# Cross-attention block on one core: the order of the work on the way into the steady loop

## The chip, the cores and the metric

The kernel runs on one core of a Trainium2 chip. The core has five engines, each with its own in-order instruction stream: TensorE (PE in the profile, matrix products, with its weight loads as PEld), VectorE (DVE), ScalarE (ACT), GpSimd (POOL) and SyncE (SP), which here only issues DMA transfers. GpSimd issues some transfers too. Engines wait for one another through semaphores. The metric is the device time of one execution in microseconds; lower is better.

## The reference

For 16 batches of 1024 rows with 512 features, the reference normalises rows, scales and shifts them by a conditioning vector, and does cross attention with 16 heads of 32 features against 64 context rows of the same batch, then projects and adds the input:

```python
xq = _ada_ln(x_q, t_vec, Wss_q, bss_q)
xkv = _ada_ln(x_kv, t_vec, Wss_kv, bss_kv)
q = (xq @ Wq + bq).reshape(B, Lq, nh, dh)
kv = (xkv @ Wkv + bkv).reshape(B, Lkv, 2, nh, dh)
scores = jnp.einsum('bqhd,bkhd->bhqk', q, k) / jnp.sqrt(jnp.float32(dh))
attn = jax.nn.softmax(scores, axis=-1)
out = jnp.einsum('bhqk,bkhd->bqhd', attn, v).reshape(B, Lq, H)
return x_q + (out @ Wp + bp)
```

`_ada_ln` is a layer norm followed by `(1 + scale) * h + bias`, where scale and bias come from `silu(c) @ W_ss + b_ss`. All is float32.

## The kernel before, in words

The 16 x 1024 rows are cut into 32 blocks of 512 rows, two per batch; a block is called by its number, counted from 0. Each block goes through these steps, each a small Python function that emits the instructions of several engines:

- `load_x(i)` (L140) fetches the rows; `q_stats` (L299) has VectorE take mean and variance; `q_scale` (L308) makes the reciprocal roots. For blocks above 2 (L281 to L288) this is five small ScalarE steps and four small GpSimd steps, "the roots". `hidden` (L328) normalises on ScalarE.
- `turn` (L497) transposes in 32 x 32 tiles on VectorE, and `move` (L510) finishes the transposition with 16 transfers, all on SP's queue or half on GpSimd's.
- Blocks 0 to 3 multiply by a query weight with the batch's scale folded in: `queries(i, o)` (L541), four steps of four matmuls, one PSUM bank each, with a bias add on ScalarE (`queried`, L557; `later=True` leaves that add to a later line). From block 4 on the features are scaled instead (`scale_features`), sums are formed on GpSimd (`feature_sums`), and seven half-size products replace eight (`query_product`, L615; Strassen's scheme). `query_seed` (L642) copies the first product from one bank to another on ScalarE, and product 2 adds onto it.
- `scores(i, z)` (L674) multiplies queries with half of the keys (z = 0 or 1), into two PSUM tiles of two banks each. Each tile is read twice: VectorE takes maxima (L698) and ScalarE copies it to a buffer (L707). The two readings of one tile exclude each other. With `crossed=True` ScalarE starts with the second tile while VectorE starts with the first. There are only two such tiles (`ps_s`), and `mix` and some key and value steps use them also, so the next step that needs one waits until both readings are done.
- `maxima` (L734) spreads the maxima over a full tile `mb` (tag "spread", one buffer), `subtract` (L740) takes them off both halves on GpSimd, `weights` (L746) is the exponential on ScalarE.
- The sums of exponentials: either `total` (L778) adds both halves on GpSimd and `row_total` (L789) sums that on VectorE, or (block 1) `sums` on each half and `halves_total`. `inverse_rows` (L803) takes the reciprocal and sends it to DRAM and back with five transfers on SP; `spread_rows` (L814) spreads what came back.
- `mix` (L839) multiplies with the values, `divided` (L822) divides on VectorE, `row_sums` (L940) forms Strassen's sums on GpSimd. Then follow seven `product` steps (L952) with the output weight into two banks, `added` (L979) after each on VectorE into the residual tile, and `biased` (L927) on ScalarE, which puts a bias into a bank before the products of that bank add to it. Products 1, 6, 5, 3 share one bank and 2, 7, 4 the other.

The schedule is manual: the order of the calls in the body is the order of instructions on every engine. A prologue, then an explicit list of calls for blocks 0 to 3 (L1000 to L1221, "the way in"), then a loop over blocks 4 to 29, then a list for the end. In the way in, the steps of up to five blocks are interleaved. `ring` says which PSUM banks of the four single ones the next steps take in turn; from L1070 on it holds only banks 0 and 1.

A tile with a tag and one buffer is shared in time: the next tile of that tag is written only after the readers of the one before it are through. `s_i_z`, the scores buffers, have the tags big0 to big3: block 3's first half has big2, and so has the sum of block 2's halves, made by `total(2)` with the line

```python
pool, tag = (xpool, "x") if i == NB - 2 else (big, f"big{(i + 1) % 2 * 2}")
```

The query tiles of blocks 2 and 3 share one buffer (tag "qt"), so the bias adds of block 3 can write it only when scores(2,1) has read block 2's.

Of the kernel before, what the change touches and what calls it, by code (L numbers as in the profile page):

```python
# [9 lines left out]
F32 = mybir.dt.float32  # L10
# [5 lines left out]
P = 128  # L16
# [4 lines left out]
def cross_attention_block(  # L21
# [58 lines left out]
    HPC = P // DH  # L80
    TB = 512
    NT = TB // P
# [12 lines left out]
    rpool = ctx.enter_context(tc.tile_pool(name="rpool", bufs=1))  # L95
    opool = ctx.enter_context(tc.tile_pool(name="opool", bufs=1))
# [12 lines left out]
    ring = [0, 1, 2, 3]  # L109
# [189 lines left out]
    def q_stats(i, ts=range(NT), kvb=None):  # L299

        if ts[0] == 0:
            q_mv[i] = small.tile([P, NT + 1, 2], F32, tag="mvq", name=f"mvq_{i}")
        for t in ts:
            row_stats(q_mv[i][:, t, :], x_tiles[i][:, t, :])
        if kvb is not None:
            row_stats(q_mv[i][:, NT, :], ctx_tiles[kvb])

    def q_scale(i, kvb=None):  # L308
        n = NT if kvb is None else NT + 1
        q_rstd[i] = rstd_of(q_mv.pop(i)[:, :n, :], n, "q", i > 2)  # L310
        if kvb is not None:
            kv_rstd[kvb] = (q_rstd[i], NT)
# [228 lines left out]
    def queries(i, o, later=False):  # L541
        xt, b = xt_tiles[i], i // BPB
        w = wq_tiles.get(b, w_q_sb)
        pq = bank(f"pq_{i}_{o}")
        for c in range(NC):
            nc.tensor.matmul(  # L546
                pq.rearrange("p (g n) -> p g n", g=4),
                lhsT=w[:, c, o * P : (o + 1) * P],
                rhs=xt[:, :, c, :],
                start=(c == 0),  # L550
                stop=(c == NC - 1),
            )
        pq_tiles[i, o] = pq
        if not later:
            queried(i, o)
# [115 lines left out]

    s_tiles, m_tiles = {}, {}

    def scores(i, z, crossed=False):  # L674

        kt, qt = k_tiles[i // BPB], qt_tiles[i]
        pss = [ps_s.tile([P, 2, TB], F32, tag="s", name=f"ps_{i}_{z}_{e}") for e in range(2)]
        for r in range(HPC):
            rows = slice(32 * r, 32 * r + 32)
            for c in range(NC):  # L680
                nc.tensor.matmul(  # L681
                    pss[r // 2][32 * c : 32 * c + 32, r % 2, :],
                    lhsT=kt[rows, c, z * HK : (z + 1) * HK],
                    rhs=qt[rows, c, :],
                    start=True,
                    stop=True,
                )
        if z == 0:
            m_tiles[i] = small.tile([P, 2, HPC, NJ], F32, tag="m2", name=f"m2_{i}")
        if i < NB - 1:  # L690
            pool, tag = big, f"big{i % 2 * 2 + z}"
        else:

            pool, tag = ((hpool, "ht"), (qpool, "xt"))[z]
        s_sb = pool.tile([P, HPC, TB], F32, tag=tag, name=f"s_{i}_{z}")

        def maximum(e):
            nc.vector.tensor_reduce(  # L698
                m_tiles[i][:, z, 2 * e : 2 * e + 2, :],
                pss[e].rearrange("p r (j a) -> p r j a", a=32),  # L700
                AX.X,
                ALU.max,
                apply_transpose=True,
            )

        def copied(e):
            nc.scalar.copy(s_sb[:, 2 * e : 2 * e + 2, :], pss[e])  # L707


        for step in (  # L710
            ((maximum, 0), (copied, 1), (maximum, 1), (copied, 0))
            if crossed
            else ((maximum, 0), (copied, 0), (maximum, 1), (copied, 1))
        ):
            step[0](step[1])
        s_tiles[i, z] = s_sb
# [33 lines left out]
    def sums(i, z):  # L750
        if z == 0:
            l_tiles[i] = small.tile([P, 2, HPC, NJ], F32, tag="l2", name=f"l2_{i}")
        nc.vector.tensor_reduce(  # L753
            l_tiles[i][:, z],
            s_tiles[i, z].rearrange("p r (j a) -> p r j a", a=32),
            AX.X,
            ALU.add,
            apply_transpose=True,
        )
# [17 lines left out]

    def total(i):  # L778

        if i == 0:  # L780

            t = opool.tile([P, HPC, TB], F32, tag="ot", name="sum_0")
        else:
            pool, tag = (xpool, "x") if i == NB - 2 else (big, f"big{(i + 1) % 2 * 2}")
            t = pool.tile([P, HPC, TB], F32, tag=tag, name=f"sum_{i}")
        nc.gpsimd.tensor_tensor(t, s_tiles[i, 0], s_tiles[i, 1], ALU.add)  # L786
        sum_tiles[i] = t
# [139 lines left out]
    def biased(i, k):  # L927

        b = b_first if k == 2 else b_diff
        k = acc_bank(i, 1 if k == 2 else 7)  # L930
        acc[k] = bank(f"pp_{i}_{k}", k)
        b = b.unsqueeze(1).to_broadcast([P, 2, HO])
        nc.scalar.copy(acc[k].rearrange("p (t h) -> p t h", t=2), b)
# [6 lines left out]
    def row_sums(i, n):  # L940

        tt = nc.gpsimd.tensor_tensor
        if n == 0:
            s1_tiles[i] = opool.tile([P, HC, HT], F32, tag="s1", name=f"s1_{i}")
            tt(s1_tiles[i], half_rows(i, 1, 0), half_rows(i, 0, 0), ALU.subtract)
            tt(half_rows(i, 1, 0), half_rows(i, 1, 1), half_rows(i, 1, 0), ALU.subtract)  # L946
        else:
            s2_tiles[i] = opool.tile([P, HC, HT], F32, tag="s2", name=f"s2_{i}")
            tt(s2_tiles[i], half_rows(i, 1, 1), s1_tiles[i], ALU.subtract)  # L949
            tt(half_rows(i, 0, 1), half_rows(i, 0, 1), s2_tiles[i], ALU.subtract)  # L950

    def product(i, n):  # L952

        rows, cols = {
            1: (lambda: half_rows(i, 0, 0), half_weights(0, 0)),
            2: (lambda: half_rows(i, 0, 1), half_weights(1, 0)),
            3: (lambda: half_rows(i, 1, 1), WT[:, 3]),
            4: (lambda: half_rows(i, 0, 1), half_weights(1, 1)),
            5: (lambda: s1_tiles.pop(i), WT[:, 0]),
            6: (lambda: s2_tiles.pop(i), WT[:, 1]),  # L960
            7: (lambda: half_rows(i, 1, 0), WT[:, 2]),
        }[n]
        rows = rows()
        k = acc_bank(i, n)
        if n == 2:
            acc[k] = bank(f"pp_{i}_{n}", k)
        for t in range(2):
            for c in range(HC):

                nc.tensor.matmul(  # L970
                    acc[k][:, t * HO : (t + 1) * HO],
                    lhsT=rows[:, c, t * P : (t + 1) * P],
                    rhs=cols[:, c, :],
                    start=n == 2 and t == 0 and c == 0,
                    stop=c == HC - 1,
                    skip_group_check=True,
                )

    def added(i, n):  # L979

        m, o = {1: (0, 0), 2: (0, 0), 6: (0, 1), 7: (1, 1), 5: (1, 1), 4: (0, 1), 3: (1, 0)}[n]
        r = r_tiles[i][:, 2 * m : 2 * m + 2, o * HO : (o + 1) * HO]
        k = acc_bank(i, n)
        a = acc[k].rearrange("p (t h) -> p t h", t=2)
        if i == NB - 1:

            for ts in ((0,), (1,)) if n == 3 else ((0, 1),):
                ts = slice(ts[0], ts[-1] + 1)
                nc.vector.tensor_add(r[:, ts, :], a[:, ts, :], r[:, ts, :])
                if n in (2, 3, 4, 5):  # L990
                    dst = rows_of(out, i)[:, 2 * m : 2 * m + 2, o * HO : (o + 1) * HO]
                    nc.sync.dma_start(dst[:, ts, :], r[:, ts, :])
            return
        nc.vector.tensor_add(r, a, r)  # L994
        if n in (3, 4):
            nc.sync.dma_start(
                rows_of(out, i)[:, 2 * m : 2 * m + 2, :], r_tiles[i][:, 2 * m : 2 * m + 2, :]
            )
# [68 lines left out]
    weights(0, 1)  # L1067
    total(0)
    move(3)
    ring[:] = [0, 1]  # L1070
    scores(1, 0, crossed=True)
    queries(2, 0)
    row_total(0)
    inverse_rows(0)
    load_x(5)
# [1 line left out]
    scores(1, 1)  # L1077
    maxima(1)
    subtract(1)
    queries(2, 1)  # L1080
    queries(2, 2)
    biased(0, 2)
    mix(0)
    spread_rows(0)
    divided(0)
    queries(2, 3)
    weights(1, 0)
    queries(3, 0, later=True)
    row_sums(0, 0)
    q_stats(4, (0, 1))  # L1090
    sums(1, 0)
    q_stats(4, (2, 3), kvb=2)
    weights(1, 1)
    product(0, 1)
    added(0, 1)
    product(0, 2)
    row_sums(0, 1)
    q_scale(4, kvb=2)
    query_weight_sums()


    scores(2, 0, crossed=True)
    added(0, 2)
    biased(0, 3)
    queries(3, 1, later=True)
    scores(2, 1)
    queried(3, 0)
    queried(3, 1)
    hidden(4, range(NT))
    maxima(2)  # L1110
    subtract(2)
# [34 lines left out]
    row_sums(1, 1)  # L1146
    q_stats(5, (3,))
    q_scale(5)
    row_total(2)
    inverse_rows(2)  # L1150
    load_residual(2)


    scores(3, 0, crossed=True)
    scale_features(4)
    feature_sums(4)
    product(1, 7)
# [161 lines left out]
    y, z = NB - 2, NB - 1  # L1319
# [134 lines left out]
```

## Time and profile before

| what | value |
|---|---|
| runs | 1042.91, 1044.82, 1045.44 us; median 1044.82 us |
| the profiled execution | 1045.25 us, of which the profiled span is 1043.3 us |
| TensorE busy | 1021.9 us, 98% of the span |
| VectorE, GpSimd, ScalarE busy | 854.4, 781.5, 610.9 us |
| mean granted TensorE clock | 0.998 |
| DMA | 147.63 MB moved, 142 GB/s |

A line of TensorE's waits reads: what waited (engine, tile, line), what it waited for (engine, tile, line), total us, number of times, the longest. A line of the timeline reads: start in us from the span's start, duration in us, engine, line, operation, output and inputs, shape, count; in brackets the idle time of the engine before it and what ended it. Rows of one kind that follow each other are merged into one. The line of the stretches gives the stretch, its sum, TensorE's busy time and count, the granted clock as a share of full speed, the share of DMA time and GB/s.

The page calls a busy TensorE busy even where its matmuls wait inside a merged row, so a row that takes longer than another of the same kind has to be looked at.

### The profile page before, as it was taken

Reading aid. Unit: us, or ns where it says so; the run is one execution under the profiler, and the core shown is the slowest. Engines: PE = TensorE matmul, PEld = TensorE weight load, DVE = VectorE, ACT = ScalarE, POOL = GpSimd, SP = SyncE. Lnnn points to the kernel's source line nnn. Section 1 sums busy time; section 2 is a strip of 40 time slices with the busy share of each in tenths; the row PEclk is TensorE's granted clock in tenths of the full one; section 3 lists DMA queues with packets and bytes.
Section 4 is the critical chain, followed back from the end, with each engine's and each line's share of the span. In section 5 each row is a group of like instructions: output and inputs, shape, how many; then the busy total and the mean of one; then the engine's idle time right before and its main releaser. Section 6 shows DMA issues by size and latency. Waiting matters only on the chain.

```text
span 1043.3 us, 22968 instructions
## 1 busy us (share of the span) xinstructions
PE 1021.9 (98%) x9058; PEld 760.0 (73%) x9058; DVE 854.4 (82%) x1159; ACT 610.9 (59%) x945; POOL 781.5 (75%) x502
## 2 busy tenths in 40 slices
PE   5999999999999999999999999999999999999998
PEld 3635686778777777777777787778787778777746
DVE  5798977987788977987878878898778997776795
ACT  3666755665567655766556666567557665565530
POOL 0479795887868868888668986688876886977861
PEclk9999999999999999999999999999999999999999
DMA  9851555444454434554335454344354444335122
GB/s 341 250 162 54 150 180 154 128 136 139 154 156 143 125 117 140 166 164 132 117 112 161 154 159 133 110 139 155 137 163 118 141 141 131 102 123 161 45 87 84
DMA packets 103499, 147.63 MB, mean 142 GB/s; under 512 B 33464, under 2 KB 34640, under 8 KB 103392
## 3 DMA queue, kind: packets, MB, share of 16 engines
q1 hardware_dynamic: 102368, 144.08, 43.5%
q0 software_dynamic: 1024, 2.10, 0.9%
q8 instruction: 71, 1.16, 0.5%
q14 instruction: 36, 0.29, 0.1%
HBM read 79.02 MB, written 34.60 MB: 109 GB/s over the span
## 4 chain that ended last, share of the span: by engine, by line
PE 91%; DVE 5%; DMA 1%; ACT 1%; POOL 1%; issue 1%; SPq 0%; DVEq 0%; ACTq 0%; POOLq 0%
PE pp L970 35%; PE pq L633 33%; PE po L855 6%; PE ps L681 6%; PE pq L546 4%; PE pv L434 3%; PE pk L398 3%; DVE m L698 1%; DMA x<-in_x_dram 1%; DVE bs L263 1%; DVE ht L503 0%; POOL s L742 0%; DVE lt L791 0%; ACT s L748 0%; DVE l L753 0%
## 5 line engine op out<-in xcount | busy, mean ns | idle before, releaser
L742 POOL TENSOR_TENSOR s<-s,mb 128x2048 f32<-128x2048 f32 x62 | 281.3, 4564 | 171.3 <-DVE mb L729 167.2
L707 ACT COPY s<-ps 128x1024 f32<-128x1024 f32 x128 | 129.4, 1012 | 112.7 <-DVE m L698 69.5
L698 DVE TRANSPOSE_TENSOR_REDUCE m<-ps 128x32 f32<-128x1024 f32 x128 | 150.8, 1215 | 31.1 <-PE ps L681 29.5
L970 PE MATMUL pp<-w_p_sb,ot 128*128 128x256 f32 x744 | 171.0, 379 | 0.9 <-DVE ot L835 0.5
L994 DVE TENSOR_TENSOR r<-pp,r 128x512 f32<-128x512 f32 x210 | 136.3, 670 | 32.1 <-PE pp L970 25.0
L663 ACT ACTIVATE qt<-pq,bias_t 128x256 f32<-128x256 f32 x224 | 92.6, 464 | 116.0 <-PE pq L633 113.3
L970 PEld LDWEIGHTS pp<-w_p_sb,ot 128*128 128x128 f32 x744 | 141.0, 190 | 21.8 <-issue 1.7
L748 ACT ACTIVATE s<-s 128x2048 f32<-128x2048 f32 x64 | 122.3, 1911 | 41.8 <-POOL s L742 40.0
L786 POOL TENSOR_TENSOR sum<-s,s 128x2048 f32<-128x2048 f32 x30 | 136.2, 4541 | 5.5 <-ACT s L748 5.5
L970 PEld LDWEIGHTS pp<-WT,s 128*128 128x128 f32 x496 | 90.6, 191 | 57.0 <-issue 35.2
L970 PE MATMUL pp<-WT,s 128*128 128x256 f32 x496 | 124.2, 394 | 0.2 <-POOL s L949 0.2
L970 PE MATMUL pp<-WT,ot 128*128 128x256 f32 x496 | 117.6, 380 | 1.0 <-POOL ot L946 0.6
L633 PE MATMUL pq<-xt_sums,wq_sums 128*128 128x256 f32 x448 | 108.5, 385 | 0.0
L633 PEld LDWEIGHTS pq<-xt_sums,wq_sums 128*128 128x128 f32 x448 | 82.9, 190 | 32.8 <-issue 21.8
L633 PE MATMUL pq<-xt,wq_sums 128*128 128x256 f32 x448 | 106.6, 381 | 0.0
L633 PE MATMUL pq<-xt,w_q_sb 128*128 128x256 f32 x448 | 106.0, 379 | 0.3 <-ACT pq L645 0.3
L970 PEld LDWEIGHTS pp<-WT,ot 128*128 128x128 f32 x496 | 93.9, 190 | 16.6 <-POOL ot L946 2.3
L324 ACT ACTIVATE x<-x,rstdq 128x512 f32<-128x512 f32 x128 | 96.6, 807 | 1.9 <-DVE rstdq L294 1.9
L670 DVE TENSOR_TENSOR qt<-pq,qt 128x256 f32<-128x256 f32 x112 | 42.0, 417 | 66.5 <-PE pq L633 66.1
L633 PEld LDWEIGHTS pq<-xt,w_q_sb 128*128 128x128 f32 x448 | 85.0, 190 | 13.1 <-ACT xt L573 0.8
L263 DVE BATCH_NORM_STATS2 bs<-x 128x6 f32<-128x512 f32 x128 | 86.9, 679 | 7.3 <-DMA x<-in_x_dram 7.3
L633 PEld LDWEIGHTS pq<-xt,wq_sums 128*128 128x128 f32 x448 | 83.5, 190 | 11.9 <-issue 1.4
(128 smaller groups left out, 1583.4 us busy)
## 6 DMA issues: line engine op xcount, KB each, us to landing
x<-in_x_dram SPq DMA_DIRECT2D x32, 1024.0 KB, 5.9
r<-in_x_dram SPq DMA_DIRECT2D x32, 1024.0 KB, 5.5
out_dram<-r SPq DMA_DIRECT2D x60, 512.0 KB, 3.7
xt<-ht SPq DMA_DIRECT2D x464, 64.0 KB, 2.0
wss_q<-in_L_xcond_Wss_q_dram SPq DMA_DIRECT2D x2, 1024.0 KB, 9.1
ctx<-in_ctx_dram SPq DMA_DIRECT2D x8, 256.0 KB, 3.1
wss_kv<-in_L_xcond_Wss_kv_dram SPq DMA_DIRECT2D x2, 1024.0 KB
w_kv_sb<-in_L_xcond_Wkv_dram SPq DMA_DIRECT2D x1, 2048.0 KB
```

The costliest lines, as they stand in the source:

```text
L263: nc.vector.bn_stats(bs, r)
L324: nc.scalar.activation(dst, src, AF.Identity, bias=rstd[:, 1, j : j + 1], scale=rstd[:, 0, j : j + 1])
L633: nc.tensor.matmul(qa[k][:, m * HT : (m + 1) * HT].rearrange("p (g n) -> p g n", g=2), lhsT=a[:, c, m * P : (m + 1) * P], rhs=x[:, :, c, : ...
L663: nc.scalar.activation(dst, src, AF.Identity, bias=bq_t[:, o : o + 1])
L681: nc.tensor.matmul(pss[r // 2][32 * c : 32 * c + 32, r % 2, :], lhsT=kt[rows, c, z * HK : (z + 1) * HK], rhs=qt[rows, c, :], start=True, s ...
L698: nc.vector.tensor_reduce(m_tiles[i][:, z, 2 * e : 2 * e + 2, :], pss[e].rearrange("p r (j a) -> p r j a", a=32), AX.X, ALU.max, apply_tra ...
L707: nc.scalar.copy(s_sb[:, 2 * e : 2 * e + 2, :], pss[e])
L742: eng.tensor_tensor(s_tiles[i, z], s_tiles[i, z], mb_tiles[i], ALU.subtract)
L748: nc.scalar.activation(p, p, AF.Exp, scale=SCALE)
L786: nc.gpsimd.tensor_tensor(t, s_tiles[i, 0], s_tiles[i, 1], ALU.add)
L970: nc.tensor.matmul(acc[k][:, t * HO : (t + 1) * HO], lhsT=rows[:, c, t * P : (t + 1) * P], rhs=cols[:, c, :], start=n == 2 and t == 0 and ...
L994: nc.vector.tensor_add(r, a, r)
```

## The change

Nothing that is computed changes. All edits lie in the way in, between about 59 and 160 us of the span:

1. `queries(2, 0)` is called ahead of `scores(1, 0)`, and so still takes a bank of the ring of four; the ring is then set to `[1, 0]`. The other three query steps of block 2 follow one call earlier each, the last of them ahead of `mix(0)`.
2. `sums(1, 0)`, one VectorE step, comes behind the maxima of `scores(2, 0)`, and the statistics of block 4 are made in one go.
3. `added(0, 2)` comes ahead of `row_sums(0, 1)` and the maxima of `scores(2, 0)`; the roots of block 4 come behind `query_weight_sums` and behind the copies of `scores(2, 0)` and the bias copy `biased(0, 3)`.
4. The bias adds of block 3's first two query steps come ahead of the copies of `scores(2, 1)`, through the new argument `first`.
5. `total(2)` puts the sum of block 2's halves into the buffer "spread" and not big2.
6. `row_total(2)`, `inverse_rows(2)` and `load_residual(2)` come behind `scores(3, 0)`.

```diff
-    def scores(i, z, crossed=False):
+    def scores(i, z, crossed=False, first=()):
...
+        for step in first:
+            queried(*step)
         if z == 0:
...
     def total(i):
-        if i == 0:
-            t = opool.tile([P, HPC, TB], F32, tag="ot", name="sum_0")
+        if i in (0, 2):
+            pool, tag = (opool, "ot") if i == 0 else (rpool, "spread")
+            t = pool.tile([P, HPC, TB], F32, tag=tag, name=f"sum_{i}")
...
     move(3)
-    ring[:] = [0, 1]
+    queries(2, 0)
+    ring[:] = [1, 0]
     scores(1, 0, crossed=True)
-    queries(2, 0)
+    queries(2, 1)
     row_total(0)
...
     subtract(1)
-    queries(2, 1)
     queries(2, 2)
+    queries(2, 3)
     biased(0, 2)
     mix(0)
     spread_rows(0)
     divided(0)
-    queries(2, 3)
     weights(1, 0)
     queries(3, 0, later=True)
     row_sums(0, 0)
-    q_stats(4, (0, 1))
-    sums(1, 0)
-    q_stats(4, (2, 3), kvb=2)
+    q_stats(4, range(NT), kvb=2)
     weights(1, 1)
     product(0, 1)
     added(0, 1)
     product(0, 2)
+    added(0, 2)
     row_sums(0, 1)
-    q_scale(4, kvb=2)
     query_weight_sums()
     scores(2, 0, crossed=True)
-    added(0, 2)
     biased(0, 3)
+    q_scale(4, kvb=2)
+    sums(1, 0)
     queries(3, 1, later=True)
-    scores(2, 1)
-    queried(3, 0)
-    queried(3, 1)
+    scores(2, 1, first=((3, 0), (3, 1)))
     hidden(4, range(NT))
...
     q_scale(5)
+    scores(3, 0, crossed=True)
     row_total(2)
     inverse_rows(2)
     load_residual(2)
-    scores(3, 0, crossed=True)
     scale_features(4)
```

## The prediction

> **What bounds the kernel now.** I read the page's busy shares first, then TensorE's waits, then the clock by stretches, then the timelines of the stage that the edits touch (59 to 160 us).
>
> ```profile
> span 1043.3 us, 22968 instructions
> ...
> PE 1021.9 (98%) x9058; PEld 760.0 (73%) x9058; DVE 854.4 (82%) x1159; ACT 610.9 (59%) x945; POOL 781.5 (75%) x502
> ```
>
> TensorE is busy 98% of the span, so a change can only win its idle time, 21.4 us, or slow periods of its clock. About 10.5 us of the idle lie before 11.3 us and 2.4 after 175 us. TensorE's waits between 40 and 175 us are what is left for this change:
>
> ```profile
> PE ps L681 <- ACT s L707: 1.9, 2, 1.3
> PE ps L681 <- DVE vt L447: 1.2, 1, 1.2
> PE pq L546 <- ACT qt L568: 0.5, 1, 0.5
> PE pp L970 <- issue: 0.4, 1, 0.4
> PE pq L633 <- ACT pq L645: 0.3, 1, 0.3
> ```
>
> The columns are total us, times, longest. The second wait is also followed by a slow clock (TensorE by stretches: us, busy, clock, DMA share, GB/s):
>
> ```profile
> 158.00:159.00 1.00, 0.00 (x0) 1.00 0.17 17
> ...
> 160.00:161.00 1.00, 1.00 (x10) 0.50 0.85 301
> ...
> 162.00:163.00 1.00, 1.00 (x3) 0.50 1.02 365
> 163.00:164.00 1.00, 1.00 (x6) 0.97 1.11 246
> ```
>
> The granted clock is halved from about 159.6 to 163.0 us: 3.4 us at half speed, 1.7 us of work lost. It is the only such place (the mean clock is 0.998).
>
> The stage where most edits meet, TensorE's timeline, then VectorE's, then ScalarE's:
>
> ```profile
> 115.76 1.14 PE L681 MATMUL ps<-qt,kt 32*32 32x512 f32 x32
> 117.33 1.97 PE L970 MATMUL pp<-WT,ot 128*128 128x256 f32 x8 [0.42 <-issue]
> ...
> 122.37 1.17 PE L681 MATMUL ps<-qt,kt 32*32 32x512 f32 x32 [1.34 <-ACT s L707]
> ...
> 127.53 1.99 PE L633 MATMUL pq<-xt,w_q_sb 128*128 128x256 f32 x8 [0.34 <-ACT pq L645]
> ```
>
> ```profile
> 117.30 2.28 DVE L791 TRANSPOSE_TENSOR_REDUCE lt<-sum 128x64 f32<-128x2048 f32 x1
> 119.61 0.55 DVE L806 RECIPROCAL lt<-lt 128x64 f32<-128x64 f32 x1
> 120.08 2.31 DVE L698 TRANSPOSE_TENSOR_REDUCE m<-ps 128x32 f32<-128x1024 f32 x2
> ```
>
> ```profile
> 125.04 1.95 ACT L707 COPY s<-ps 128x1024 f32<-128x1024 f32 x2
> 126.88 0.59 ACT L645 COPY pq<-pq 128x512 f32<-128x512 f32 x1
> ```
>
> VectorE has no pause from 115.9 to 141.8 us: there it is as full as TensorE.
>
> **Hand-over times**, read from rows. A scores step keeps TensorE 1.07 us; the maxima of its first bank can start 1.19 us after its first matmul (87.19 to 88.38), the copy of its second after 1.35 (43.34 to 44.69). A whole query product takes 3.63, its bias add may start 3.74 after its start (97.15 to 100.89). A half-size product takes 1.73 to 1.83; its addition may start about 1.9 after its start. Maxima 1.2, copy 1.0, spread 2.31 each. Maxima and copy of one bank exclude each other.
>
> **First part, 59.6 to 97 us: queries(2,·) around scores(1,·).** Now scores(1,0) starts at 59.62 and the next step at 61.96: 2.34 us instead of 1.07, because the last bias add of block 1 (60.16, behind an exponential on ScalarE) is late. Then scores(1,1) waits 0.57 for copies. Changed: queries(2,0) covers 59.62 to 63.25 (its features and weights are there by 53); scores(1,0) 63.25; queries(2,1) to 67.95; its copies end at 66.7 and maxima at 66.8, so scores(1,1) goes on. Gain 1.27+0.57 = 1.84. Without that cover the copies (66.7) against 64.3 would cost 2.4. queries(2,2) and (2,3) reach 76.08, mix(0) 78.36, queries(3,0) 81.9, where block 3's features (last issue 71.6, 2.6 to land) are ready. VectorE's division of block 0 starts at 78.39 (mix start + 2.31) instead of 78.26: 0.13, hidden under queries(3,0). Products 1 and 2 run from 81.9 to 85.45, scores(2,0) 85.45, queries(3,1) 86.52 to 90.15, scores(2,1) 90.15.
>
> Order on VectorE: five statistics (0.8 each) to 84.65, added(0,1) and now added(0,2) to 86.2, maxima 86.64 to 89.2 (the second waits for the copy that follows weights(1,1), 87.0 to 88.0), then sums(1,0), now behind them, to 91.5, maxima of scores(2,1) to 93.9, spread to 96.5 (98.2 before). ScalarE: copies to 89.0, b_diff copy 89.6, five roots to 90.9; queried(3,0) and (3,1) have to wait for scores(2,1) to have read the same buffer, 91.5 to 92.75, then the copies to 94.9. So queries(3,2) finds its bank free and starts at 94.8 instead of 97.15: the 0.47 wait goes too, **−2.3** in all. On GpSimd the weight sums now come ahead of the roots' four small steps (1.1): hidden(4) may start at 96.45, not 94.9, and turn(4) needs it only at 101.6, so that costs nothing. subtract(2) starts at 96.6 (98.35 before).
>
> **Second part, 97 to 119 us: sum_2 in the "spread" buffer, row_total(2) behind scores(3,0).** VectorE is 1.65 ahead: sums(1,1) ends at 100.0, the reciprocal at 100.85; its way through DRAM takes 4.66 as now (102.5 to 107.16), to 105.5; division of block 1 at 107.9. TensorE: mix(1) 103.69, queries(3,3) to 109.5, products to 113.4, scores(3,0) 113.45. product(1,7) needs the b_diff copy (114.85) and row_sums on GpSimd (subtract(2) to 105.65, weights(2,1) 107.75, total 112.4, two steps: 115.0), so it starts at 115.2 and scores(3,1) at 118.8. In the old form the copy into big2 waited for row_total(2) to read that buffer (119.66) and scores(3,1) could start only at 122.37. Here the lead is 3.6.
>
> **Third part, where that lead is lost.** row_total(2) and its reciprocal (2.78) have not left VectorE, they stand behind. The first maxima start at 115.0; the second bank's wait for its copy, which is behind five roots on ScalarE (115.2 to 116.35): 117.4 to 118.6, 1.2 idle. Then row_total and reciprocal to 121.35, added(1,7) and (1,6) to 122.6, maxima of scores(3,1) to 125.0, second copy 126.0, seed copy 126.55. Queued behind row_total are thus two additions, four maxima and through them the seed that query_product(4,2) waits for: it starts at 126.6 instead of 127.53, **−0.95**. TensorE has query_product(4,1) from 119.9, waits 1.0 for added(1,6), runs product(1,5), and waits 2.1 for the seed: 3.1 us idle where there were 1.7. The moved inverse_rows also sends five small transfers and the load of r_2 later on SP's queue: first transfer at 121.5 instead of 120.19; it lands behind x_6 (issued 117.0, 5.9 us: 123), the rest by 127.4; spread_rows(2) wants them at 128.2, so 0.8 is to spare. Block 4's move is 16 issues, 106 to 116.7, landed by 118.9, in time for its scaling; r_2 lands by 134, wanted at 139.
>
> **Fourth part, 127 to 160 us.** TensorE has no wait till scores(4,0), VectorE keeps its 0.95: turn(5) ends at 139.45, load_x(7) lands as now 6.0 later, statistics of block 7 at 145.5 to 148.7, one addition to 149.45. row_total(3) had to wait 1.33 for GpSimd; now subtract(3) begins at 127.7 (130.49 before), the sum is ready at about 149.1, and no wait is left. From row_total's start to the last value tile is 7.1 us (151.72 to 158.85): 156.55. The second half of scores(4,0), wanted at 156.3, starts at 156.7 instead of 159.0: **−2.3** (0.95 and two effects of 0.4 to 0.9: the gap shrinks from 1.2 to 0.4).
>
> **The clock.** The gap at 158 is gone, so I take the slow window away: **−1.7**. From 163 us on TensorE sets the pace again and a lead at scores(4,1) is kept: VectorE had 4.4 us idle there. Sum: −2.3−1.7 = −4.0, bounds −1.0 (both clock terms bad) and −5. The profiled execution took 1045.25 us (1.95 around its span), so 1041.25, **1041.3**. Against the runs' median, 1044.82, this is −0.34%; those runs lie between 1042.91 and 1045.44, and the lowest may be one without a slow window.
>
> The rule that speaks against it: this trace halves the clock after a gap of 1.2 us (beside scores, whose matmuls are 32x32), but not after 1.34 at 122.37. [...]
>
> **The rivals.** (a) The new idle time halves the clock: 1042.65, 1041.8 to 1043.8, chance 0.28. For: the row at 160. Against: the larger gap without it at 122. (b) The gain isn't there: the roots ahead of the copy hold VectorE longer than 1.2 us, the seed comes at 127.5 as now and the gap and slow clock at 158 stay: 1045.2, chance 0.12. For: VectorE's full row. Against: it is fed 1.65 to 2.3 earlier. (c) Slower: the small transfers of inverse_rows(2) are caught behind bulk loads, spread_rows(2) blocks VectorE's queue with the division of block 2, turn(5) and load_x(7) behind it. Each us beyond 128.2 counts; with the lead of 4.0 used up and 3.1 more, it decides from about 7 us of lateness: 1048.5, chance 0.14. For: such a transfer took 4.8 us behind a load at 120. Against: 9 us from reciprocal to use now.
>
> **How the numbers follow.** The main case has 0.46, with its own range 1040.2 to 1042.4. A measurement of this kernel tells about 0.3%, 3.1 us: faster is below 1041.7, slower above 1048.0. Faster: 0.40 of the main case and 0.04 of (a): 0.44. Same: 0.06+0.24+0.12 = 0.42. Slower 0.14. The range leaves out (c) and some of each end: 1040.0 to 1045.4.
>
> **What would show it.** Right: queries(3,2) near 94.8; scores(3,1) near 118.8 with no wait for L791's buffer; a wait of about 2 us before query_product(4,2) near 126.6; scores(4,0) without a 1.2 us gap; no halved clock at 160. Wrong if the clock row shows a halved stretch between 124 and 132, if spread_rows(2) waits for its transfer, if row_total(3) still waits for GpSimd, or if TensorE shows new waits after 165 us.

## The result and the profile after

| | before | changed |
|---|---|---|
| median of 13 runs each, us | 1045.17 (1042.88 to 1046.55) | 1040.9 (1039.77 to 1043.3) |
| ratio to before, with 95% interval | | 0.9965 (0.9956 to 0.9975) |
| profiled execution, us | 1045.25, span 1043.3 | 1040.31, span 1038.5 |

The changed kernel is faster by 0.35%. The forecast was 1041.3 us. The executions of the kernel before lie in two groups, about 1043 and 1045.5 us (here 5 and 8 of 13), so a ratio to it depends on how many fall into each; the experiments show that it is the clock of TensorE (a mean of 0.998 and less in the upper group, of 0.999 and more in the lower).

After the change TensorE is busy for 1019.3 of 1038.5 us. Its waits from 40 to 175 us:

```profile
PE pq L633 <- ACT pq L645: 1.8, 1, 1.8
PE pp L976 <- POOL ot L952: 0.6, 1, 0.6
PE pq L633 <- ACT xt L573: 0.3, 1, 0.3
```

All the old waits for a scores tile are gone; what has grown is the wait for the seed copy (L645), 1.8 us instead of 0.3. The first part, TensorE before: the two steps of scores(1,·), of which the first is cut in two by a wait, and queries(3,2):

```profile
59.62 1.05 PE L681 MATMUL ps<-qt,kt 32*32 32x512 f32 x6
60.88 1.13 PE L681 MATMUL ps<-qt,kt 32*32 32x512 f32 x26 [0.21 <-ACT qt L568]
...
66.22 1.18 PE L681 MATMUL ps<-qt,kt 32*32 32x512 f32 x32 [0.57 <-ACT s L707]
...
97.15 3.70 PE L546 MATMUL pq<-xt,wq 128*128 128x512 f32 x8 [0.47 <-ACT qt L568]
```

The same after, without a wait:

```profile
61.78 1.14 PE L684 MATMUL ps<-qt,kt 32*32 32x512 f32 x32
...
66.48 1.14 PE L684 MATMUL ps<-qt,kt 32*32 32x512 f32 x32
...
93.31 3.60 PE L546 MATMUL pq<-xt,wq 128*128 128x512 f32 x8
```

TensorE's timeline in the stage where the edits meet, to be held against the four lines shown of before:

```profile
112.46 1.14 PE L684 MATMUL ps<-qt,kt 32*32 32x512 f32 x32
...
117.86 1.14 PE L684 MATMUL ps<-qt,kt 32*32 32x512 f32 x32
...
121.52 1.99 PE L976 MATMUL pp<-WT,s 128*128 128x256 f32 x8
125.34 1.99 PE L633 MATMUL pq<-xt,w_q_sb 128*128 128x256 f32 x8 [1.83 <-ACT pq L645]
```

VectorE at the same time, and ScalarE's copies and seed:

```profile
114.09 1.22 DVE L703 TRANSPOSE_TENSOR_REDUCE m<-ps 128x32 f32<-128x1024 f32 x1
116.29 1.25 DVE L703 TRANSPOSE_TENSOR_REDUCE m<-ps 128x32 f32<-128x1024 f32 x1 [0.98 <-ACT s L712]
117.47 2.27 DVE L797 TRANSPOSE_TENSOR_REDUCE lt<-sum 128x64 f32<-128x2048 f32 x1
...
120.24 1.22 DVE L1000 TENSOR_TENSOR r<-pp,r 128x512 f32<-128x512 f32 x2
```

```profile
122.65 2.14 ACT L712 COPY s<-ps 128x1024 f32<-128x1024 f32 x2 [1.33 <-DVE m L703]
124.69 0.59 ACT L645 COPY pq<-pq 128x512 f32<-128x512 f32 x1
```

The row sum of block 2 (L797) stands between the two pairs of maxima, and ahead of it VectorE waits 0.98 us for a copy. Both were forecast. At scores(4,0) the gap between the two halves of the step is down from 1.22 us, before:

```profile
156.69 1.09 PE L681 MATMUL ps<-qt,kt 32*32 32x512 f32 x16
159.00 1.42 PE L681 MATMUL ps<-qt,kt 32*32 32x512 f32 x16 [1.22 <-DVE vt L447]
```

to 0.16 after:

```profile
154.51 1.09 PE L684 MATMUL ps<-qt,kt 32*32 32x512 f32 x16
155.75 1.09 PE L684 MATMUL ps<-qt,kt 32*32 32x512 f32 x16 [0.16 <-PE ps L684]
```

The idle time of these rows understates the gap. In a step without a gap the second half starts 0.45 us after the first (e3 below, and every other scores step of the changed kernel); at scores(4,0) it starts 2.31 us after it before and 1.24 in this profile. So the second half is late by 1.9 us before and still by 0.8 after.

The clock stays full both there and beside the wait for the seed (columns as in the prediction):

```profile
124.00:126.00 2.00, 0.66 (x3) 1.00 0.17 16
...
156.00:160.00 4.00, 4.00 (x31) 1.00 0.85 295
```

**A ruler for small differences.** From the first `mix` behind scores(4,1) on, the starts of successive `mix` steps were compared over eight profiles of different kernels: the same 29.2, 29.6, 32.8 and 33.0 us recur, step by step within 0.2 us. What differs from one profile to the next outside the way in is the start (the first scores step began at 42.0 to 43.6 us) and the last stores (from the last mix step to the end 21.4 to 23.4 us over seven of them). So I count from the first matmul of scores(0,0) to the first one of three later steps. This takes the start and the end out, and leaves the way in:

| kernel | to queries(3,2) | to query_product(4,2) | to scores(4,1) | clock halved in the profile | executions with a halved stretch | ratio to before |
|---|---|---|---|---|---|---|
| before | 53.81 | 84.19 | 121.98 | yes, 3.4 us | 23 of 60 | 1 |
| changed | 51.25 | 83.28 | 118.36 | no | 0 of 13 | 0.9965 |
| e5, changed again | 51.25 | 82.69 | 117.31 | no | 0 of 8 | 0.9973 |
| e1, edits 1 to 4 | 51.25 | 81.91 | 118.03 | no | 0 of 8 | 0.9974 |
| e2, edits 5 and 6 | 54.00 | 85.38 | 120.23 | no | 0 of 11 | 0.9990 |
| e9, edit 1 | 52.83 | 83.21 | 120.96 | yes, 3.4 us | 9 of 10 | 0.9996 |
| e10, edits 2 to 4 | 53.20 | 83.48 | 119.61 | no | 9 of 10 | 1.0003 |
| e3, before, gap closed | 53.82 | 84.20 | 118.17 | no | 0 of 9 | 0.9975 |
| e4, changed, roots later | 51.25 | 81.68 | 117.10 | no | 0 of 5 | 0.9965 |
| e8, e4 and values earlier | 51.25 | 81.50 | 115.47 | no | 0 of 5 | 0.9958 |
| e6, gap made longer | 53.84 | 84.22 | 124.49 | yes, 6.8 us | 4 of 4 | 1.0041 |
| e7, seed made later | 51.26 | 84.13 | 120.53 | yes, 3.4 us | 8 of 10 | 0.9991 |

The last column but one is read from the mean granted clock of each execution. In the profile of before the clock is 0.50 from 159.64 to 163.06 us; such a stretch of 3.41 us takes 1.7 of some 1043 us, or 0.0016, off the mean, so 0.998 and less are counted as halved. The clock also falls behind the last matmul of the program: in the profile of the changed kernel that one ends at 1034.81 us, and the clock is 0.95 from 1037.00 to 1038.50. The eight profiles without a halved stretch have a mean of 0.999 or 1.000. The 60 executions of before are those on the three chips of the experiments.

For a halved stretch of 3.41 us I take off 1.7, half of its length: an estimate, which the rows bear out (the second half of scores(4,0) and the product behind it take 1.42 and 3.32 us in before, 1.09 and 2.00 in e1 at full clock, 1.65 less). So before without it is 120.28. The two profiles of the changed kernel are 1.9 and 3.0 us below that. Three profiles of the kernel before agree within 0.04 us (121.95 to 121.99), the two of the changed kernel differ by 1.05.

### The profile page after: what moved, and what is told of

It is laid out like the page before. It is cut to its first block, busy times and chain, and to the rows that moved or that the text cites. A ratio compares the mean times of both kernels' runs of the same rounds, so it can differ in the third digit from the quotient of the medians.

```text
span 1038.5 us, 22968 instructions
## 1 busy us (share of the span) xinstructions
PE 1019.3 (98%) x9058; PEld 759.5 (73%) x9058; DVE 854.9 (82%) x1159; ACT 610.6 (59%) x945; POOL 780.9 (75%) x502
## 3 DMA queue, kind: packets, MB, share of 16 engines
q8 instruction: 72, 1.18, 0.5%
## 4 chain that ended last, share of the span: by engine, by line
PE 84%; DVE 7%; DMA 3%; POOL 3%; ACT 1%; issue 1%; SPq 0%; DVEq 0%; POOLq 0%
PE pp L976 34%; PE pq L633 33%; PE po L861 6%; PE ps L684 6%; PE pv L434 2%; PE pk L398 2%; DMA x<-in_x_dram 2%; DVE m L703 1%; DVE bs L263 1%; DVE l L758 1%; DVE vb L823 1%; DVE lt L797 1%; DMA vr<-ltd 1%; DVE ot L841 1%; DVE r L1000 0%
```

## The experiments

### Which edits carry the gain

**e1_order_only.** The changed kernel with edits 5 and 6 taken back:

```diff
-        if i in (0, 2):
+        if i == 0:
...
-    scores(3, 0, crossed=True)
     row_total(2)
     inverse_rows(2)
     load_residual(2)
+    scores(3, 0, crossed=True)
```

> The changed kernel with its edits 5 and 6 undone: the sum of block 2 is in big2 again, and row_total(2) with its transfers stands ahead of scores(3,0) again. Theory A (the order edits 1 to 4 carry the gain, and VectorE sets the pace between 110 and 126 us, so moving row_total only moves the wait): the copies of scores(3,0) wait for row_total(2) again, scores(3,1) waits about 1.2 us for them, but VectorE loses no time waiting for a copy; from queries(3,2) to query_product(4,2) it takes about 30.9 us (32.0 in the changed kernel, 30.4 in the one before), and the time is 0 to 1 us below the changed kernel's, near 1040. Rival B (the buffer and the later row_total carry a good part): 1042.5 to 1043.5.

Measured: 0.9974 (0.9964 to 0.9983), median 1041.23 us against 1043.81 of before on that chip. TensorE waits at scores(3,1) again, but the seed is there earlier than in the changed kernel (84.19 − 81.91 = 2.3 us won, against 0.9 and 1.5 in its two profiles); from queries(3,2) to query_product(4,2) it takes 30.66 us. TensorE's waits:

```profile
PE ps L684 <- ACT s L712: 1.3, 1, 1.3
PE ps L684 <- DVE vt L447: 1.2, 1, 1.2
...
PE pq L633 <- ACT pq L645: 0.3, 1, 0.3
```

The time is that of the changed kernel, not the 1 us below it which I allowed for: the gap at scores(4,0) is back (1.18 us) and uses the earlier seed up. Edits 1 to 4 alone are worth the whole change, as far as intervals of about 1 us to either side can tell.

**e2_buffer_only.** Edits 5 and 6 alone on the kernel before:

```diff
-        if i == 0:
...
+        if i in (0, 2):
+            pool, tag = (opool, "ot") if i == 0 else (rpool, "spread")
...
+    scores(3, 0, crossed=True)
     row_total(2)
     inverse_rows(2)
     load_residual(2)
...
-    scores(3, 0, crossed=True)
```

> The kernel before with edits 5 and 6 alone: the sum of block 2 in the spread buffer, row_total(2) behind scores(3,0). Theory A: the wait of 1.34 us before scores(3,1) goes, but the seed copy comes 1.3 us later, because row_total now stands between the two pairs of maxima and VectorE also waits for a copy; from queries(3,2) to query_product(4,2) 31.7 us instead of 30.4. The gap at scores(4,0) shrinks since TensorE is late itself, so the time is 1043.5 to 1045.5, by whether the clock is then halved. Rival B: 1042 to 1043, 2 to 3 us faster than before.

Measured: 0.9990 (0.9982 to 0.9999), median 1043.34. The wait before scores(3,1) is gone, and the seed is 1.2 us later (85.38 against 84.19; expected 1.3): the moved row sum only changes what TensorE waits for. TensorE comes later to scores(4,0) and finds no idle time there, and none of 11 executions has a halved stretch, against 8 of 23 of before on that chip. That is the whole of the small rest: the 15 executions of before at full clock have a median of 1043.44, e2 one of 1043.34, and to scores(4,1) the two take the same, 120.23 and 120.28.

**e9_queries_only.** Edit 1 alone on the kernel before:

```diff
-    ring[:] = [0, 1]
+    queries(2, 0)
+    ring[:] = [1, 0]
     scores(1, 0, crossed=True)
-    queries(2, 0)
+    queries(2, 1)
...
-    queries(2, 1)
     queries(2, 2)
+    queries(2, 3)
...
     divided(0)
-    queries(2, 3)
```

> The kernel before with edit 1 alone (queries(2,0) ahead of scores(1,0), the other three one call earlier). From the first matmul of scores(0,0) to that of queries(3,2) it took 53.8 us before and 51.3 in the changed kernel. Theory (the two groups of order edits need each other: TensorE gains 1.8 us at scores(1,0) and scores(1,1), but VectorE's old order takes part of it back at scores(2,0) and scores(2,1)): 52.8 to 53.0 here, and to scores(4,1) 119.3 us, against 120.3 before without the halved clock and 118.0 with all of edits 1 to 4. Rival (edit 1 does it all): 51.5 to 52.0, and 118.3.

Measured: 52.83 us to queries(3,2), 1.0 of the 2.6 that the changed kernel wins there; and 119.26 us to scores(4,1) when the 1.7 of its halved stretch are taken off 120.96. The old order behind TensorE's takes back the rest: scores(2,1) waits 0.88 us for the copies of scores(2,0). They stand behind block 4's roots on ScalarE, which waited 0.75 us for the statistics that VectorE makes behind sums(1,0):

```profile
90.28 1.47 PE L681 MATMUL ps<-qt,kt 32*32 32x512 f32 x32 [0.88 <-ACT s L707]
```

The ratio, 0.9996 (0.9985 to 1.0008), shows no gain, but the clock hides it: 9 of 10 executions are halved, against 8 of 19 of before on that chip. At halved clock the medians are 1043.72 and 1045.48 us.

**e10_rest_only.** Edits 2 to 4 alone: e1 with the four query steps where they were before.

```diff
-    queries(2, 0)
-    ring[:] = [1, 0]
+    ring[:] = [0, 1]
     scores(1, 0, crossed=True)
-    queries(2, 1)
+    queries(2, 0)
...
     subtract(1)
+    queries(2, 1)
     queries(2, 2)
-    queries(2, 3)
...
     divided(0)
+    queries(2, 3)
```

> The kernel before with edits 2 to 4 alone (sums, additions, roots, bias adds ahead of the copies; the queries stay). Theory: only the wait of 0.47 us before queries(3,2) goes, the distance from scores(0,0) to queries(3,2) is 53.2 to 53.4; the spread of block 2's maxima comes as before, since scores(2,1) comes as before, so to scores(4,1) it takes 119.9 to 120.3 us without a halved clock. Rival (edits 2 to 4 do it all): 51.5 to 52.0, and 118.3.

Measured: 53.20 us to queries(3,2), and 119.61 to scores(4,1), a little better than expected; 1.0003 (0.9990 to 1.0016). Here too 9 of 10 executions are halved, though not the profiled one; the nine have a median of 1044.51 against 1045.48 of before at halved clock. The singles win 1.0 and 0.7 us of way in (120.28 − 119.26 and 120.28 − 119.61), both together 2.25 (e1: 120.28 − 118.03), each read from one profile: edit 1 brings scores(2,0) and scores(2,1) earlier on TensorE, and only the new order on VectorE can take them up.

**e4_roots_later.** The changed kernel, and the five roots of block 5 behind the copies of scores(3,0):

```diff
-    q_scale(5)
     scores(3, 0, crossed=True)
+    q_scale(5)
     row_total(2)
```

> The changed kernel with one more move: the roots of block 5 stand behind the copies of scores(3,0) on ScalarE. Theory A: VectorE's wait of 1.0 us for the copy of scores(3,0)'s second tile goes, the seed copy and all of VectorE's work up to load_x(7) come 1.0 us earlier; from queries(3,2) to query_product(4,2) 31.0 us instead of 32.0, the time 1.0 us below the changed kernel's, about 1039.9. Rival (TensorE's 1.8 us wait for the seed is covered later anyhow): the wait shrinks to 0.8 but the time stays at 1040.9.

Measured: the 0.98 us of VectorE are gone (its two maxima are one row again), and the seed comes 1.0 to 1.6 us earlier than in the two profiles of the changed kernel:

```profile
114.95 2.35 DVE L703 TRANSPOSE_TENSOR_REDUCE m<-ps 128x32 f32<-128x1024 f32 x2
117.22 2.27 DVE L797 TRANSPOSE_TENSOR_REDUCE lt<-sum 128x64 f32<-128x2048 f32 x1
```

TensorE's wait for the seed shrinks to 1.16 us, but a gap of 0.50 opens at scores(4,0), whose second half is 1.1 us late (it starts 1.58 after the first), and the ratio, 0.9965 (0.9953 to 0.9977), cannot be told from the changed kernel's. So whether the 1.0 us shows in the time is left open.

### The gap, the seed and the clock

**e3_gap_closed.** The kernel before with one move:

```diff
+    value_products(2, spare("pv_2"))
+    value_tiles(2)
     turn(6, range(NT))
     load_x(8)
-    value_products(2, spare("pv_2"))
-    value_tiles(2)
```

> The kernel before with one move: value_products(2) and value_tiles(2) are called ahead of turn(6), so VectorE frees the second PSUM tile about 2.4 us earlier and scores(4,0) has no gap of 1.2 us. Theory (the gap beside the scores step makes the clock fall): no halved stretch near 160 us in the profile, and the median falls by 1.2 for the gap and up to 1.7 for the clock, to 1042.3 to 1043. Rival (the halved stretch has another cause, and comes by chance): 1.2 us less only, 1044, with halved stretches still there in the longer runs.

Measured: 0.9975 (0.9965 to 0.9985), median 1041.35; scores(4,0) runs without a gap and the clock is full. To query_product(4,2) it is the kernel before (84.20 us), to scores(4,1) it is 2.1 us below it, on top of the halved stretch. That is more than the 1.2 us that were expected for the gap, and the median is below the 1042.3 to 1043 forecast: the second half of the step now starts 0.45 us after the first, not 2.31, so the gap had cost 1.9 and not the 1.2 of its row. At full clock before has 1043.44 on that chip, again 2.1 above. This one move, which the change does not make, is worth about as much as the change.

**e6_gap_at_scores.** The kernel before, with two transposes of block 6 done twice, which makes VectorE 1.2 us later at the value tiles:

```diff
-        for t in ts:
+        for t in [*ts, 2, 3] if i == 6 else ts:
             nc.vector.transpose(
```

> The kernel before with turn(6) transposing its last two tiles twice, 1.2 us more on VectorE ahead of the value tiles: the gap inside scores(4,0) becomes 2.4 us. Theory (idle time beside the scores step lets the clock fall): the clock is halved for 3.4 us right after it, and the time is 1.2 us above the kernel before plus up to 1.7 for the executions of that one that keep their clock, so 1.2 to 2.9. [...]

Measured: slower, 1.0041 (1.0025 to 1.0057), 1048.31 against 1043.42 us. The gap is 2.41 us, and the clock is halved not for 3.4 us but for 6.8, from 159.2 to 166.0 (columns as before):

```profile
156.37 1.09 PE L681 MATMUL ps<-qt,kt 32*32 32x512 f32 x16
159.87 1.96 PE L681 MATMUL ps<-qt,kt 32*32 32x512 f32 x16 [2.41 <-DVE vt L447]
```

```profile
159.00:160.00 1.00, 0.13 (x8) 0.58 0.00 0
160.00:161.00 1.00, 1.00 (x16) 0.50 0.21 55
...
165.00:166.00 1.00, 1.00 (x4) 0.51 0.57 109
```

1.2 us more on VectorE cost 4.9 by the medians, more than the 1.2 to 2.9 expected, since before is mostly at full clock there (11 of 18 executions) and every execution of e6 is halved, three of four at a mean clock of 0.997.

**e7_gap_at_seed.** The changed kernel, the first maxima of scores(3,1) taken twice:

```diff
             step[0](step[1])
+            if (i, z) == (3, 1) and step == (maximum, 0):
+                step[0](step[1])
```

> The changed kernel with the first maxima of scores(3,1) taken twice, 1.2 us more on VectorE ahead of the seed copy: TensorE's wait for the seed grows from 1.8 to 3.0 us, among full-size matmuls. VectorE's chain sets the end of the way in, so the time is about 1.2 us above the changed kernel's. [...]

Measured: 0.9991 (0.9982 to 1.0001), median 1043.08, which is 1.8 above the changed kernel on that chip, where about 1.2 was expected. The clock falls in 8 of 10 executions; these have a median of 1043.29, and the two at full clock took 1042.54 and 1042.58: halving seems to cost less than 1.7 us of the time here, and with two executions that is not settled. With 3.11 us of wait for the seed the clock is halved from 128.2 to 131.6 us:

```profile
127.04 2.69 PE L633 MATMUL pq<-xt,w_q_sb 128*128 128x256 f32 x8 [3.11 <-ACT pq L645]
```

```profile
128.00:129.00 1.00, 1.00 (x4) 0.59 1.05 399
...
130.00:131.00 1.00, 1.00 (x4) 0.50 0.05 18
```

**e11_before_again, e12_before_again.** The kernel before, unaltered, for two more profiles.

> The kernel before, unaltered, for another profile. The executions of it lie in two groups, about 1043 and 1045.5 us. Theory (the gap of 1.2 us at scores(4,0) lets the clock fall only in some executions): either a halved stretch of 3.4 us at about 159 and a time near 1045.5, or full clock and a time near 1043; the gap is there in both. Rival: a halved stretch elsewhere, or none in an execution of 1045.5.

> As e11_before_again: one more sample of the kernel before. The gap at scores(4,0) is 1.2 us; halved clock and about 1045.5 us, or full clock and about 1043 us.

Measured: 1045.54 and 1045.57 us, both with the gap (1.19 and 1.21 us) and a halved clock. In e11 the stretches show it from 159.3 us on, for 3.4 us; in e12 the mean clock is 0.998, and the second half of scores(4,0) and the product behind it take 1.34 and 3.38 us (1.09 and 2.00 in e1). With the first one that is three of three, all in the upper group; no profile caught one of the lower group. But the mean clock of every execution shows that the groups are the clock's: on the three chips the executions with a mean clock of 0.999 and more have medians of 1043.44, 1043.27 and 1042.92 us (15, 11 and 11 of them), those with less 1045.46, 1045.69 and 1045.48 (8, 7 and 8). They lie 2.0 to 2.6 us apart; 1.7 of that, by the estimate above, is the halved stretch, and what the rest is was not found.

### Again, and better

**e5_changed_again.** The changed kernel, unaltered, beside e6, e7 and e8.

> The changed kernel, unaltered, beside the other runs on one chip. Its first profile started 1.3 us earlier than that of the kernel before for reasons ahead of the change; counted from the first matmul of scores(0,0) to that of scores(4,1), it took 118.4 us against 122.0 before, of which 1.7 was the halved clock. If the order alone counts, this distance is 118.4 again, with no halved clock, and the ratio to before 0.9965 to 0.9975; if the first profile was a lucky one, the distance is 119 or more or a halved stretch shows between 124 and 132 us.

Measured: 0.9973 (0.9962 to 0.9984), median 1041.27; no halved stretch. The way in took 117.31 us, 1.05 less than in the first profile; neither of the two expected outcomes, 118.4 or 119 and more. In both, spread_rows(0) waits for its transfers, which it did not before (1.27 us in the first profile, 0.74 in this one); later steps on VectorE are late by what is left of it. The ratio depends on how many runs of before fall into its upper group: 8 of 13 in the first comparison, 7 of 18 in this one. Against the 11 executions of before at full clock (1043.27) the changed kernel is 2.0 us faster.

**e8_roots_and_values.** e4 and the move of e3 together:

> The changed kernel with the roots of block 5 behind the copies of scores(3,0) and value_products(2), value_tiles(2) ahead of turn(6). The first move alone took the distance from scores(0,0) to scores(4,1) from 118.4 to 117.1 us and left a gap of 0.5 at scores(4,0). Theory: the gap goes, 116.6 us, and the time is 1.5 to 1.8 below the changed kernel's. Rival: with the gap gone the maxima of scores(4,0), now behind turn(6), hold up scores(4,1), and nothing is won over the first move alone.

Measured: 0.9958 (0.9946 to 0.9971), median 1039.16, 2.1 us below the changed kernel on that chip, a little more than expected. All its executions are below all of the changed kernel's there. From scores(0,0) to scores(4,1) it takes 115.47 us, where 116.6 was expected; the first move alone took 117.10. Here too the gap at scores(4,0) had cost more than the 0.50 of its row.

## Why the prediction was right

**The lead of the first part** was put at 2.3 us; it is 2.56 (53.81 − 51.25), and 51.25 to 51.26 in every kernel with edits 1 to 4. The two groups of edits do need each other, as the step by step account had it (VectorE's order behind TensorE's): alone they give 1.0 and 0.6 of the 2.56.

**The lead at scores(3,1)** was put at 3.6; in the first profile it is 3.23 (79.03 before, 75.80 after, from scores(0,0)).

**Its loss** was the step on which the sum hung, and it held: 0.95 forecast at query_product(4,2), 0.91 measured in the first profile and 1.50 in the second. The wait for the copy behind the roots was put at 1.2 and is 0.98, the wait for the seed at 2.1 and is 1.83. Of the 1.0 us that TensorE was to wait for added(1,6) at most 0.4 came: product(1,5) starts 2.26 us after query_product(4,1), which takes 1.83. e1 and e2 show the cause by taking buffer and row sum away and adding them alone, e4 by moving the roots; buffer and row sum were not parted. What the prediction did not say, though its own sums give it, is that edits 5 and 6 add nothing.

**The fourth part** was put at 2.3; in the first profile the second half of scores(4,0) starts 1.97 earlier (115.66 before, 113.69 after) and scores(4,1) 1.92 without the clock; in the second it is 3.0 for both. The term that was mis-sized is the 0.13 us at the division of block 0: the transfers ahead of it landed late and VectorE waited 1.27 and 0.74 in the two profiles. The forecast that the second half of scores(4,0) comes 0.4 late lies between the 0.8 and 0.3 of the two profiles; before it was 1.9 late, not the 1.2 of the row which the prediction took for it. Neither row_total(3) nor spread_rows(2) waited, and the 0.8 us to spare for the latter's transfers were about 0.7, an estimate: the last of them was issued at 124.75, the first landed 1.5 after its issue, and they were wanted at 126.92.

**The clock** gave the 1.7 that the sum took for it, in this profile; over the runs of before it is a share of that, by how many fall into the upper group. That 8 of 13 did in this comparison, so that the median of before stood where the profiled execution had been, is luck: on the three chips of the experiments it was 23 of 60, the medians of before were 1043.42 to 1043.99, and e5 is 2.15 below its one. The forecast of 1041.3 against the profiled 1045.25, −4.0, stands against −3.6 for the way in of the two profiles; the rest of the difference of the two spans (−4.8) is a start that came 1.3 us earlier and has nothing to do with the change.

**The rivals.** (a), a halved clock beside the seed, did not happen at 1.8 us of wait in any of 21 executions, and e7 shows it at 3.1. How near it was between these was not tested. The time lost to it that stands in 1042.65 is shown by no run: in e7 the eight executions with a halved clock have a median 0.7 us above that of the two without (1043.29 and 1042.56). (b) and (c) did not happen.

## What to carry to other kernels

Where two engines are both full, taking a wait from one can win little or nothing unless the other's order is changed with it (e2 nothing, e9 1.0 of 2.6 us); add up what stands ahead of the next hand-over on the second engine before a lead is believed. A lead that arrives early at a wait is lost there (e1 has 2.3 us at the seed, the changed kernel 0.9 and 1.5, and the two the same time), and the last wait of the stage (here a PSUM tile freed by the value tiles) decides. To compare small edits, count from one instruction to another inside the trace, so that first loads and last stores drop out, and compare whole times only between executions of the same mean clock: e9 and e10 show no gain against all executions of before, and 1.8 and 1.0 us against those at halved clock.

## What was not expected of the hardware

A longer wait of TensorE was not always followed by a halved clock, nor a shorter one by a full clock. Ten waits of over 1.1 us, with the idle time of the row and the mean clock of the profile:

| profile | wait before | idle, us | mean clock | clock behind it | executions halved |
|---|---|---|---|---|---|
| before | scores(3,1) | 1.34 | 0.998 | full | |
| before | second half of scores(4,0) | 1.22 | 0.998 | halved from 159.64, 3.4 us | 23 of 60 |
| e11 | the same | 1.19 | 0.998 | halved from 159.3, 3.4 us | |
| e12 | the same | 1.21 | 0.998 | halved, by the rows | |
| e9 | the same | 1.18 | 0.998 | halved, by the rows | 9 of 10 |
| e10 | the same | 1.20 | 0.999 | full | 9 of 10 |
| e1 | the same | 1.18 | 0.999 | full | 0 of 8 |
| e6 | the same | 2.41 | 0.997 | halved from 159.2, 6.8 us | 4 of 4 |
| changed | query_product(4,2) | 1.83 | 1.000 | full | 0 of 13 |
| e7 | query_product(4,2) | 3.11 | 0.998 | halved from 128.2, 3.4 us | 8 of 10 |

Idle time by rows does not sort them: 1.18 was halved, 1.83 was not. It would be natural to say that 32x32 matmuls beside the gap count for less than full-size ones. But the profiles of e1 and e10 have the same 32x32 matmuls around the same gap and keep the full clock, and in that of before TensorE runs 32x32 matmuls alone from 988.17 to 992.97 us, with a clock of 1.00. So they alone did not bring the fall in these profiles.

So the same gap costs 1.7 us or nothing, and what decides it was not shown. It is not evenly spread, though: with gaps of 1.18 to 1.22 us none of 8 executions of e1 was halved, 23 of 60 of before, and 9 of 10 each of e9 and e10. In their profiles this gap ends 113.4, 115.7, 114.7 and 114.9 us after scores(0,0) began, so the share may follow its place in the program; that was not tested.
